# Two score products against one: the row maximum carried in spare rows of a matmul, with a full product ahead of it

## The chip, the cores and the metric

The kernel runs on one core of one Trainium2 chip. A core has a matrix engine (PE), a vector engine (DVE), a scalar engine that evaluates functions (ACT), a general engine (POOL, GpSimd), a queue that issues transfers (SP) and 16 DMA engines. Each has its own in-order instruction queue, and they meet through semaphores. The metric is device time in microseconds (us). All numbers are fp32.

## The reference, cut to what matters

A decoder of two layers works on 32 sequences of 128 tokens and width 128, each with its own context of 77 vectors. Each layer has a mixing step over the sequence, a cross-attention to the context and a mixture of experts, and a layer norm behind each. The change touches only the second layer's cross-attention, a differential attention with 16 heads, two queries and two keys of 4 dimensions per head, so 32 softmaxes per token:

```python
q = (query @ Wq.T).reshape(B, Nq, 2 * H, HD).transpose(0, 2, 1, 3)
k = (key_ @ Wk.T).reshape(B, Nk, 2 * H, HD).transpose(0, 2, 1, 3)
v = (value @ Wv.T).reshape(B, Nk, H, 2 * HD).transpose(0, 2, 1, 3)
a1 = softmax(q1 @ k1 * SCALE) @ v          # the first H of 2H heads
a2 = softmax(q2 @ k2 * SCALE) @ v          # the other H
attn = a1 - lam * a2                        # then normalised per head, scaled, @ Wp.T + bp
```

Each softmax takes the maximum of its 77 scores off before the exponential.

## The kernel before

The 32 sequences are handled in 8 groups of 4 (`G`). Everything is written with a tile framework: the Python code calls engines in an order of its own, generators are woven (`weave`, `beside`) so that parts of several stages alternate, and the framework then places each instruction in its engine's queue by priority and adds the semaphores. What stands first in a queue holds up what is behind it.

The second cross-attention is `cross1`, one generator over all 32 sequences (items). `beside(crossing, 6 * G, ...)` runs 24 steps of it per group and lets `before1(g + 1)` (gathering the experts' output in `combined`, the `memory` stage, then `prepare1`) and `after1(g - 1)` (`joined1`) take steps between. With group 2 done, the second half of the first layer's sorted experts is put in between (about 1010 to 1150 us).

`prepare1` makes, per group: the transposed queries (`dpq` in PSUM, copied by ACT to `dqT`, L753), the transposed keys (`dpk`, copied to `dkT`, L757), and per item the keys spread eight times with a mask (`km`, L763, on POOL): row group w (32 partitions) holds 8 of the 32 softmaxes, 4 rows each, and copy u of the keys is zero outside the 4 rows of softmax u. So copies 0 to 3 are zero in rows 16 to 31 of each row group, copies 4 to 7 in rows 0 to 15. The key dimension is padded from 77 to 78 by repeating the last one. `values` (L427, L435) makes the value operands `vb`.

An item passes through these steps, each for one half k (4 of the 8 softmaxes of each row group):

- `scores(n, k)`: four products (L784), one per row group, into four banks of PSUM; four DVE reductions (L786) write the maxima into `tops`, 8 used columns of 32 per row group.
- `by_query(n)`: PE transposes `tops` (`pt_mx`, L795), ACT copies it to `mT` (L797): now row 32w + u holds the maximum of softmax u for each query.
- `weights(n, k, mT)`: for each of three key thirds t and four row groups w, a product of keys and queries (L808, 32x104 stationary), and then, added onto the same place, a product (L819) of a constant selector `fold` (−1 where a key column belongs to softmax u) and `mT`. The sum is score minus maximum, keys on partitions. It lies in two PSUM tiles of two banks each (`dst`, pool `pair`, two buffers). ACT takes the exponential, one instruction per tile (L136 through `expln`, out `pT`).
- `reads(n, pTs, lhs, out)`: 12 products (L836) with `vb` or the mask `vmask` give numerators and denominators (`pav`), the item before being read while the present one is weighed.
- `difference`: reciprocal as exp(−ln) on ACT (`rd`), two DVE operations.

The PSUM pool `bank` has four buffers, shared by `dsc`, `pt_mx`, `dpq`, `dpk`, `pvc`, `pav` and others. The `prob` pool holds three `km` tiles of two items each.

Of the kernel before, what the change touches and what calls it, by code (L numbers as in the profile page):

```python
# [17 lines left out]
P = 128  # L18
# [33 lines left out]
def shape_constants():  # L52
    p = np.arange(P)
    cols = {}
    cols["ident"] = np.eye(P)
    cols["ones"] = np.ones((P, P))
    cols["before"] = (p[:, None] < p[None, :]) * 1.0
    cols["blk16"] = (p[:, None] // 16 == p[None, :] // 16) / 16.0
    cols["lag"] = np.maximum(p[None, :] - 1 - p[:, None], 0)
    cols["parity"] = np.broadcast_to(  # L60
        ((p[None, :] // 16) % 2 == np.arange(2)[:, None]).reshape(1, 2 * P), (P, 2 * P)
    )
    cols["qmask"] = (p[:, None] % 32) // 16 == np.arange(2)[None, :]
    cols["kmask0"] = ((p[:, None] % 32) // 8 == np.arange(4)[None, :]) / np.sqrt(8.0)
    cols["kmask1"] = ((p[:, None] % 32) // 4 == np.arange(8)[None, :]) * 0.5

    head, key = np.minimum(p // KT, 4), p % KT
    own = (head[:, None, None] == (np.arange(P) % 32 // 8)[None, None, :]) & ~(
        (np.arange(3) == 2)[None, :, None] & (key == KT - 1)[:, None, None]
    )  # L70
    cols["vmask"] = own.reshape(P, 3 * P)

    cols["fold"] = np.concatenate([p[:, None] % 32 == 4 * k + np.arange(4 * KT)[None, :] // KT for k in range(2)], axis=1) * -1.0
    cols["blk8"] = (p[:, None] // 8 == p[None, :] // 8) / 8.0
    cols["iota8"] = np.broadcast_to(np.arange(NE)[None, :], (P, NE))
    cols["iota32"] = np.broadcast_to(np.arange(32)[None, :], (P, 32))
    cols["before16"] = (p[:, None] // 16 == p[None, :] // 16) & (p[:, None] < p[None, :])
    cols["lower16"] = (p[:, None] // 16 < p[None, :] // 16) / 16.0
    cols["tile_no"] = np.broadcast_to(np.arange(NT)[None, :], (P, NT))
    cols["quad"] = p[:, None] // 32 == np.arange(4)[None, :]  # L80

    cols["token"] = p[:, None] + P * (2 * np.arange(16)[None, None, :] + np.arange(2)[None, :, None]).reshape(1, B)
    cols["eps"] = np.full((P, 1), EPS)
    at, parts, n = {}, [], 0
    for name, v in cols.items():
        v = np.asarray(v, np.float32)
        at[name] = (n, n + v.shape[1])
# [19 lines left out]
def kernel(ctx: ExitStack, tc: tile.TileContext, a: dict, at: dict):  # L107
# [57 lines left out]
    def c_(name):  # L165
        return cst[:, at[name][0] : at[name][1]]
# [6 lines left out]
        return vec[:, i : i + 1]  # L173

    ident, ones = c_("ident"), c_("ones")
    dmat = cp.tile([P, 8, P], F32, name="dmat")
    wv = cp.tile([P, 2, P], F32, name="wv")
    rows = cp.tile([P, 2, P], F32, name="rows")
# [568 lines left out]
    def prepare1(g, x4, c4):  # L747
        xT = transposed(x4, "c1")
        yield
        pq = bank("dpq")  # L750
        nc.tensor.matmul(pq, lhsT=w_("L1_xattn_Wq"), rhs=xT.rearrange("p b s -> p (b s)"), start=True, stop=True)
        qT = wk.tile([P, G, S], F32, tag="qT", name="dqT")
        nc.scalar.copy(qT, pq.rearrange("p (b s) -> p b s", b=G))  # L753
        pk = bank("dpk")[:, : G * S2]
        nc.tensor.matmul(pk, lhsT=w_("L1_xattn_Wk"), rhs=c4[:, :, 0, :], start=True, stop=True)
        kT = wk.tile([P, G, S2], F32, tag="ckT", name="dkT")
        nc.scalar.copy(kT, pk.rearrange("p (b k) -> p b k", b=G))  # L757
        yield
        km, vbs = [], []
        for b0 in range(0, G, 2):  # L760
            pair_km = wk.tile([P, 2, 8, S2], F32, tag="prob", bufs=3, name="km1")
            for i in range(2):
                nc.gpsimd.tensor_tensor(  # L763
                    pair_km[:, i],
                    kT[:, b0 + i, :].unsqueeze(1).broadcast_to([P, 8, S2]),
                    c_("kmask1").unsqueeze(2).broadcast_to([P, 8, S2]),
                    ALU.mult,
                )
                km.append(pair_km[:, i])
            for i in range(2):  # L770
                vbs.append(values(c4, b0 + i, 1))
            yield
        oT = wk.tile([P, G, S], F32, tag="oT", name="oT1")
        for b in range(G):
            operands[g * G + b] = qT[:, b, :], km[b], vbs[b], oT[:, b, :]
        held["oT", g] = oT

    def scores(n, k):

        qT, km, _, _ = operands[n]  # L780
        banks = [bank("dsc") for _ in range(4)]
        for w in range(4):
            rr = slice(32 * w, 32 * w + 32)
            nc.tensor.matmul(banks[w][:, : 4 * S2], lhsT=qT[rr], rhs=km[rr, 4 * k : 4 * k + 4, :], start=True, stop=True)  # L784
        for w in range(4):
            nc.vector.tensor_reduce(  # L786
                tops[n % 3][:, w, 4 * k : 4 * k + 4],
                banks[w][:, : 4 * S2].rearrange("p (h k) -> p h k", h=4),
                AX.X,
                ALU.max,  # L790
            )

    def by_query(n):
        pm = bank("pt_mx")[:, :P]
        nc.tensor.transpose(pm, tops[n % 3].rearrange("p w u -> p (w u)"), ident)  # L795
        mT = wk.tile([P, P], F32, tag="mT", name="mT")
        nc.scalar.copy(mT, pm)  # L797
        return mT

    def weights(n, k, mT):  # L800
        qT, km, _, _ = operands[n]
        pT = wk.tile([P, 2, 2, 3, S], F32, tag="pT", bufs=4, name="pT1")
        pts = [pair("dst") for _ in range(2)]
        fold = c_("fold")[:, k * 4 * KT : (k + 1) * 4 * KT]
        for t in range(3):
            for w in range(4):
                rr = slice(32 * w, 32 * w + 32)
                nc.tensor.matmul(  # L808
                    pts[w // 2][: 4 * KT, w % 2, t * S : (t + 1) * S],
                    lhsT=km[rr, 4 * k : 4 * k + 4, :].rearrange("p h k -> p (h k)")[:, t::3],  # L810
                    rhs=qT[rr],
                    start=(t == 0),
                    stop=False,
                    skip_group_check=True,
                )
        for t in range(3):
            for w in range(4):
                rr = slice(32 * w, 32 * w + 32)
                nc.tensor.matmul(  # L819
                    pts[w // 2][: 4 * KT, w % 2, t * S : (t + 1) * S],  # L820
                    lhsT=fold[rr],
                    rhs=mT[rr, :],
                    start=False,
                    stop=(t == 2),
                    skip_group_check=True,
                )
        for m in range(2):
            expln(pT[: 4 * KT, m].rearrange("p r t s -> p r (t s)"), pts[m][: 4 * KT, :, : 3 * S], AF.Exp)
        return pT
# [22 lines left out]
    def cross1():  # L852

        for n, k in ((0, 0), (0, 1), (1, 0)):
            scores(n, k)
            yield
        mT, past = by_query(0), None
        for n in range(B):
            pTs = [weights(n, 0, mT)]
            yield  # L860
            if past:
                acc = bank("pav1").rearrange("p (n m s) -> p n m s", n=2, m=2)
                reads(n - 1, past, operands[n - 1][2], acc[:, 0])
            yield
            if n + 1 < B:
                scores(n + 1, 1)
            yield
            pTs.append(weights(n, 1, mT))
            yield
            if past:  # L870
                reads(n - 1, past, vmask, acc[:, 1])
                difference(n - 1, acc)
            yield
            if n + 1 < B:
                mT = by_query(n + 1)
            if n + 2 < B:
                scores(n + 2, 0)
            yield
            past = pTs
        acc = bank("pav1").rearrange("p (n m s) -> p n m s", n=2, m=2)  # L880
        reads(B - 1, past, operands[B - 1][2], acc[:, 0])
        reads(B - 1, past, vmask, acc[:, 1])
        difference(B - 1, acc)
# [425 lines left out]
```

## Time and profile before

| what | value |
|---|---|
| three runs | 1725.04, 1725.79, 1734.47 us; median 1725.79 us |
| profiled execution | 1722.96 us, span 1721.2 us, mean granted PE clock 0.785 |
| PE busy (matmul) | 1309.1 us, 76% of the span |
| PE weight loads | 960.2 us, 56% |
| DVE / ACT / POOL busy | 767.3 (45%) / 461.1 (27%) / 544.0 (32%) us |
| instructions | 27680 |
| 882 to 985 us, PE busy, granted clock | 95.60 us, 0.96 |
| 1150 to 1470 us, PE busy, granted clock | 276.55 us, 0.88 |

How to read it: a line of the groups view has the code line, the engine, the operation, output<-inputs, shapes, the count, busy time and mean nanoseconds, and then the engine's idle time ahead of these instructions with what ended it. A timeline line has start, duration, engine, line and count, and in brackets the idle time before with its releaser. A window line has the stretch, its length, the busy time of PE, weight loads, DVE, ACT and POOL with counts, the granted PE clock as a share of full speed, the DMA share and GB/s. Each fp32 product of this kernel leaves two matmul records. Matmuls overlap, so that the sum of their durations is not the time PE is held; starts of neighbours tell that.

### The profile page before, as it was taken

The numbers are of one execution on the slowest core, as the hardware profiler recorded it, in microseconds if no ns is written. First come the engines' busy times: TensorE is split into PE (matmuls) and PEld (weight loads), VectorE is DVE, ScalarE is ACT, GpSimd is POOL, SyncE is SP. The second block draws the span as 40 slices with busy tenths as digits, with TensorE's granted clock in tenths as the row PEclk, the third lists the DMA queues.
The fourth block names the chain that finished last, engine by engine and source line by source line (L and its number), as shares of the span: only waits on it lengthen the run. The fifth ranks groups of instructions, "written<-read, shape, count | busy, mean of one in ns | idle before, by whom it ended". The sixth has DMA issues, their size and how long they took to land. (4 is left out here: it accounts for less than half of the span.)

```text
span 1721.2 us, 27680 instructions
## 1 busy us (share of the span) xinstructions
PE 1309.1 (76%) x11537; PEld 960.2 (56%) x11537; DVE 767.3 (45%) x2107; ACT 461.1 (27%) x928; POOL 544.0 (32%) x437
## 2 busy tenths in 40 slices
PE   5778877785677999678669999987889999425940
PEld 3555554554455888456336678865656666225520
DVE  3655556553555222676225532225355353472212
ACT  2222222221132333223023433323324333100213
POOL 0532424346643111652821101125121010004662
PEclk7966666666576999877679999998889998555885
DMA  8000000102200454110221026541110000001234
GB/s 244 20 22 19 20 18 21 26 11 70 80 19 7 144 186 151 50 34 25 82 70 35 14 71 195 172 137 44 28 40 14 16 14 14 16 0 27 54 30 109
DMA packets 122254, 100.98 MB, mean 59 GB/s; under 512 B 50064, under 2 KB 110224, under 8 KB 122128
## 3 DMA queue, kind: packets, MB, share of 16 engines
q1 hardware_dynamic: 105776, 50.30, 10.6%
q0 software_dynamic: 16352, 48.91, 9.9%
q8 instruction: 91, 1.49, 0.4%
q14 instruction: 35, 0.29, 0.1%
HBM read 72.29 MB, written 26.89 MB: 58 GB/s over the span
## 5 line engine op out<-in xcount | busy, mean ns | idle before, releaser
L669 PE MATMUL pgu<-tT,wt 128*128 128x256 f32 x736 | 172.0, 382 | 1.7 <-ACT tT L648 1.7
L786 DVE TENSOR_REDUCE top<-dsc 128x4 f32<-128x312 f32 x256 | 111.7, 475 | 122.8 <-PE dsc L784 115.5
L136 ACT ACTIVATE pT<-dst 104x768 f32<-104x768 f32 x128 | 96.7, 807 | 255.0 <-PE dst L819 205.0
L675 DVE TENSOR_TENSOR sg<-sg,pgu 128x512 f32<-128x512 f32 x92 | 63.3, 688 | 194.9 <-ACT sg L136 194.9
L669 PEld LDWEIGHTS pgu<-tT,wt 128*128 128x128 f32 x736 | 135.8, 192 | 18.2 <-ACT tT L648 2.2
L507 PE MATMUL ptp<-cst,prob 128*104 128x128 f32 x384 | 89.5, 410 | 73.3 <-POOL prob L497 60.6
L784 PE MATMUL dsc<-km,dqT 32*128 32x312 f32 x512 | 113.9, 503 | 29.6 <-DVE top L786 27.2
L494 POOL TENSOR_TENSOR prob<-prob,z 128x1248 f32<-128x1248 f32 x32 | 90.6, 2830 | 107.3 <-DVE z L493 103.1
L507 PEld LDWEIGHTS ptp<-cst,prob 128*104 128x104 f32 x384 | 70.8, 201 | 94.8 <-POOL prob L497 65.8
L808 PE MATMUL dst<-dqT,km 32*104 32x128 f32 x1536 | 117.4, 336 | 5.0 <-ACT pT L136 2.4
L654 POOL DMA_INDIRECT wt<-in_experts,which x46 | 43.9, 955 | 239.5 <-PE pd L679 226.9
L808 PEld LDWEIGHTS dst<-dqT,km 32*104 32x104 f32 x1536 | 97.6, 227 | 16.5 <-issue 7.4
L679 PE MATMUL pd<-wt,sg 128*128 128x128 f32 x736 | 99.6, 278 | 2.5 <-DVE sg L675 0.8
L679 PEld LDWEIGHTS pd<-wt,sg 128*128 128x128 f32 x736 | 93.1, 191 | 13.5 <-DVE sg L675 8.4
L784 PEld LDWEIGHTS dsc<-km,dqT 32*128 32x128 f32 x512 | 48.1, 195 | 79.0 <-DVE top L786 51.2
L819 PE MATMUL dst<-mT,cst 32*104 32x128 f32 x1536 | 87.0, 295 | 4.5 <-issue 4.4
L496 DVE TENSOR_REDUCE mx<-prob 128x16 f32<-128x1248 f32 x32 | 46.4, 1451 | 87.1 <-POOL prob L494 87.1
L497 POOL TENSOR_TENSOR prob<-prob,mx 128x1248 f32<-128x1248 f32 x32 | 72.9, 2279 | 38.4 <-DVE mx L496 36.6
L698 POOL DMA_INDIRECT two<-yslot,place x64 | 63.2, 988 | 67.7 <-DVE facc L705 29.7
L836 PE MATMUL pav<-pT,cst 104*32 104x256 f32 x768 | 65.6, 407 | 22.5 <-issue 21.7
L136 ACT ACTIVATE sg<-pgu 128x512 f32<-128x512 f32 x92 | 55.0, 597 | 95.5 <-PE pgu L669 95.5
L819 PEld LDWEIGHTS dst<-mT,cst 32*104 32x104 f32 x1536 | 77.0, 181 | 6.4 <-issue 6.4
(304 smaller groups left out, 2454.2 us busy)
## 6 DMA issues: line engine op xcount, KB each, us to landing
c<-in_ctxT SPq DMA_DIRECT2D x64, 156.0 KB
xslot<-zero SPq DMA_DIRECT2D x22, 256.0 KB
xs<-xslot SPq DMA_DIRECT2D x22, 256.0 KB
yslot<-y SPq DMA_DIRECT2D x22, 256.0 KB
wt<-in_experts SPq DMA_DIRECT2D x4, 768.0 KB
xg<-in_x SPq DMA_DIRECT2D x8, 256.0 KB
accrow<-fh SPq DMA_DIRECT2D x8, 256.0 KB
facc<-accrow SPq DMA_DIRECT2D x8, 256.0 KB
```

Of the source, the lines that this page charges most:

```text
L136: act = nc.scalar.activation(out, x, func, **kw)
L494: nc.gpsimd.tensor_tensor(ph, ph, z, ALU.add)
L497: nc.gpsimd.tensor_tensor(ph, ph, mx.unsqueeze(2).broadcast_to([P, 16, S2]), ALU.subtract)
L507: nc.tensor.transpose(pt[: 4 * KT, i, t * S : (t + 1) * S], ph[:, h0 : h0 + 4, :].rearrange("p h k -> p (h k)")[:, t::3], ident,)
L669: nc.tensor.matmul(pgu[:, i, c * TB * P : (c + 1) * TB * P], lhsT=w[:, at_w : at_w + P], rhs=x, start=True, stop=True)
L675: nc.vector.tensor_mul(flat, flat, pgu[:, 1, :])
L679: nc.tensor.matmul(pd[:, b, :], lhsT=sg[:, c, b, :], rhs=w[:, at_w : at_w + D], start=(c0 + c == 0 and b == 0), stop=(c0 + c == I0 // P - ...
L784: nc.tensor.matmul(banks[w][:, : 4 * S2], lhsT=qT[rr], rhs=km[rr, 4 * k : 4 * k + 4, :], start=True, stop=True)
L786: nc.vector.tensor_reduce(tops[n % 3][:, w, 4 * k : 4 * k + 4], banks[w][:, : 4 * S2].rearrange("p (h k) -> p h k", h=4), AX.X, ALU.max,)
L808: nc.tensor.matmul(pts[w // 2][: 4 * KT, w % 2, t * S : (t + 1) * S], lhsT=km[rr, 4 * k : 4 * k + 4, :].rearrange("p h k -> p (h k)")[:, t ...
L819: nc.tensor.matmul(pts[w // 2][: 4 * KT, w % 2, t * S : (t + 1) * S], lhsT=fold[rr], rhs=mT[rr, :], start=False, stop=(t == 2), skip_group ...
L836: nc.tensor.matmul(out[js], lhsT=lhs[: 4 * KT, t, js], rhs=pTs[j % 2][: 4 * KT, :, j // 2, t, :], start=(t == 0), stop=(t == 2), skip_grou ...
```

## The change

`weights` does one product in place of two. The masked keys `km` get −1 in one of the rows that were zero (a new constant `minus`), in row 16(1−k) + u mod 4; the queries are kept twice, each zeroed outside one half's 16 rows (`qz`, two ACT operations from PSUM), the maxima go to the matching columns of `tops`, and `by_query` adds the transposed maxima, masked to the other half's rows, to each half's queries (`qa`, two DVE operations straight from PSUM, in place of ACT's copy). So a row of −1 meets the row of the maximum within the same product. The key copies, with their scale and the −1 as bias, are made by ACT, 8 operations of 128x78 per item, in place of one POOL operation of 128x624. Ahead of each call's products, `busy` writes a product of the identity and 512 constant columns into the call's first bank; the real products overwrite what is read. The selector `fold` (208 columns) leaves the constants.

```diff
-    cols["fold"] = np.concatenate([p[:, None] % 32 == 4 * k + np.arange(4 * KT)[None, :] // KT for k in range(2)], axis=1) * -1.0
+    cols["minus"] = (p[:, None] % 32 == 16 * (1 - np.arange(8)[None, :] // 4) + np.arange(8)[None, :] % 4) * -1.0
...
+    def busy(banks):
+
+        for out in banks:
+            nc.tensor.matmul(out, lhsT=ident, rhs=cst[:, :512], start=True, stop=True)
...
-        qT = wk.tile([P, G, S], F32, tag="qT", name="dqT")
-        nc.scalar.copy(qT, pq.rearrange("p (b s) -> p b s", b=G))
+        qz = []
+        for k, tag in enumerate(("qT", "rq")):
+            qz.append(wk.tile([P, G, S], F32, tag=tag, name=f"dq{k}"))
+            nc.scalar.activation(
+                qz[k], pq.rearrange("p (b s) -> p b s", b=G), AF.Identity, bias=0.0, scale=c_("qmask")[:, k : k + 1]
+            )
...
-                nc.gpsimd.tensor_tensor(
-                    pair_km[:, i],
-                    kT[:, b0 + i, :].unsqueeze(1).broadcast_to([P, 8, S2]),
-                    c_("kmask1").unsqueeze(2).broadcast_to([P, 8, S2]),
-                    ALU.mult,
-                )
+                for u in range(8):
+                    nc.scalar.activation(
+                        pair_km[:, i, u, :], kT[:, b0 + i, :], AF.Identity,
+                        bias=c_("minus")[:, u : u + 1], scale=c_("kmask1")[:, u : u + 1],
+                    )
...
-            nc.tensor.matmul(banks[w][:, : 4 * S2], lhsT=qT[rr], rhs=km[rr, 4 * k : 4 * k + 4, :], start=True, stop=True)
+            nc.tensor.matmul(banks[w][:, : 4 * S2], lhsT=qz[k][rr], rhs=km[rr, 4 * k : 4 * k + 4, :], start=True, stop=True)
...
-                tops[n % 3][:, w, 4 * k : 4 * k + 4],
+                tops[n % 3][:, w, 16 * (1 - k) : 16 * (1 - k) + 4],
...
-        mT = wk.tile([P, P], F32, tag="mT", name="mT")
-        nc.scalar.copy(mT, pm)
-        return mT
+        qa = wk.tile([P, 2, P], F32, tag="mT", name="qa")
+        for k in range(2):
+            nc.vector.scalar_tensor_tensor(qa[:, k, :], pm, c_("qmask")[:, 1 - k : 2 - k], qz[k], ALU.mult, ALU.add)
+        return qa
...
         pts = [pair("dst") for _ in range(2)]
-        fold = c_("fold")[:, k * 4 * KT : (k + 1) * 4 * KT]
+        busy([pts[0][:, 0, :]])
         for t in range(3):
             for w in range(4):
                 rr = slice(32 * w, 32 * w + 32)
                 nc.tensor.matmul(
                     pts[w // 2][: 4 * KT, w % 2, t * S : (t + 1) * S],
                     lhsT=km[rr, 4 * k : 4 * k + 4, :].rearrange("p h k -> p (h k)")[:, t::3],
-                    rhs=qT[rr],
-                    start=(t == 0),
-                    stop=False,
-                    skip_group_check=True,
-                )
-        for t in range(3):
-            for w in range(4):
-                rr = slice(32 * w, 32 * w + 32)
-                nc.tensor.matmul(
-                    pts[w // 2][: 4 * KT, w % 2, t * S : (t + 1) * S],
-                    lhsT=fold[rr],
-                    rhs=mT[rr, :],
-                    start=False,
-                    stop=(t == 2),
-                    skip_group_check=True,
+                    rhs=qa[rr, k, :],
+                    start=True,
+                    stop=True,
                 )
```

More of the change, by code (lines that the diff above doesn't have):

```diff
@@ L774, in prepare1 @@
         for b in range(G):
-            operands[g * G + b] = qT[:, b, :], km[b], vbs[b], oT[:, b, :]
+            operands[g * G + b] = [q[:, b, :] for q in qz], km[b], vbs[b], oT[:, b, :]
         held["oT", g] = oT
     def scores(n, k):
-        qT, km, _, _ = operands[n]
+        qz, km, _, _ = operands[n]
         banks = [bank("dsc") for _ in range(4)]
@@ L793, in by_query, with weights @@
     def by_query(n):
+        qz, _, _, _ = operands[n]
         pm = bank("pt_mx")[:, :P]
         nc.tensor.transpose(pm, tops[n % 3].rearrange("p w u -> p (w u)"), ident)
-        mT = wk.tile([P, P], F32, tag="mT", name="mT")
-        nc.scalar.copy(mT, pm)
-        return mT
-    def weights(n, k, mT):
-        qT, km, _, _ = operands[n]
+        qa = wk.tile([P, 2, P], F32, tag="mT", name="qa")
+        for k in range(2):
+            nc.vector.scalar_tensor_tensor(qa[:, k, :], pm, c_("qmask")[:, 1 - k : 2 - k], qz[k], ALU.mult, ALU.add)
+        return qa
+    def weights(n, k, qa):
+        _, km, _, _ = operands[n]
         pT = wk.tile([P, 2, 2, 3, S], F32, tag="pT", bufs=4, name="pT1")
         pts = [pair("dst") for _ in range(2)]
-        fold = c_("fold")[:, k * 4 * KT : (k + 1) * 4 * KT]
+        busy([pts[0][:, 0, :]])
         for t in range(3):
@@ L856, in cross1 @@
             yield
-        mT, past = by_query(0), None
+        qa, past = by_query(0), None
         for n in range(B):
-            pTs = [weights(n, 0, mT)]
+            pTs = [weights(n, 0, qa)]
             yield
@@ L867, in cross1 @@
             yield
-            pTs.append(weights(n, 1, mT))
+            pTs.append(weights(n, 1, qa))
             yield
@@ L874, in cross1 @@
             if n + 1 < B:
-                mT = by_query(n + 1)
+                qa = by_query(n + 1)
             if n + 2 < B:
```

## The prediction

> **What bounds the kernel now.** I read the page's 40 slices first, to find the stage that the change touches. The tiles `dst`, `dsc` and `pT1` of the second cross-attention run from 770 to 1465 us, with the first layer's second half of sorted experts in the middle, and the rest of the kernel is untouched except for a constant. The costliest groups name what is removed:
>
> ```profile
> L808 PE MATMUL dst<-dqT,km 32*104 32x128 f32 x1536 | 117.4, 336 | 5.0 <-ACT pT L136 2.4
> L819 PE MATMUL dst<-mT,cst 32*104 32x128 f32 x1536 | 87.0, 295 | 4.5 <-issue 4.4
> L136 ACT ACTIVATE pT<-dst 104x768 f32<-104x768 f32 x128 | 96.7, 807 | 255.0 <-PE dst L819 205.0
> ```
>
> Each product leaves two records (64 calls of 12 products are 768, the rows say 1536). ScalarE's exponentials wait 205 us for PE and hardly the reverse: PE sets the pace. Its share from 1230 to 1465 us is 214.5 of 235 us, at a granted clock of 0.90. So I went to PE's timeline of one quiet half of an item (one `scores`, one `weights`, one `reads`):
>
> ```profile
> 1362.16 0.80 PE L784 MATMUL dsc<-km,dqT 32*128 32x312 f32 x6
> 1363.53 0.53 PE L784 MATMUL dsc<-km,dqT 32*128 32x312 f32 x1 [0.56 <-DVE top L786]
> 1363.53 0.56 PE L808 MATMUL dst<-dqT,km 32*104 32x128 f32 x6
> 1363.89 0.42 PE L784 MATMUL dsc<-km,dqT 32*128 32x312 f32 x1
> 1363.92 0.92 PE L808 MATMUL dst<-dqT,km 32*104 32x128 f32 x16
> ...
> 1365.72 1.50 PE L836 MATMUL pav<-pT,cst 104*32 104x256 f32 x24
> ```
>
> A half lasts about 5.1 us. See that the 4th score product and the first `dst` product start at the same 1363.53: they use different groups of 32 rows and run side by side. From there to the next stage, both products of `weights` take 2.19 us.
>
> **Part 1, the second product goes and a full one comes.** What 24 L819 records cost is best seen where `dst` follows a full product, and so is the price of `busy`:
>
> ```profile
> 1401.38 0.79 PE L784 MATMUL dsc<-km,dqT 32*128 32x312 f32 x2 [0.56 <-DVE top L786]
> 1402.10 1.97 PE L427 MATMUL pvc<-wv,c 128*104 128x128 f32 x12
> 1404.00 0.85 PE L808 MATMUL dst<-dqT,km 32*104 32x128 f32 x16
> 1404.68 0.83 PE L819 MATMUL dst<-mT,cst 32*104 32x128 f32 x24
> 1405.44 0.85 PE L836 MATMUL pav<-pT,cst 104*32 104x256 f32 x12
> ```
>
> ```profile
> 1246.10 1.02 PE L889 MATMUL prms<-sq,cst 128*128 128x512 f32 x2
> 1247.05 1.50 PE L836 MATMUL pav<-pT,vb 104*32 104x256 f32 x24
> ```
>
> L819 fills 1404.68 to 1405.44: 0.76 us. A full 128x512 product holds PE from 1246.10 to 1247.05: 0.95 us, 0.96 in another place. So the trade alone loses 0.20 us per call. In the quiet half it loses more, because the full product needs all rows: in the first fence here the next full product starts 1402.10 − 1401.38 = 0.72 us after the last score product, while `dst` starts after 0.00. The Trainium skill (TensorEngine Tiling, section Key Properties) says that a change of tiling mode drains the engine, which speaks against this change. By the naive sum a half would gain or lose only 0.96 − 0.76 = +0.20; with the drain it is 0.72 (drain) + 0.96 + 1.02 (24 L808 records from a fresh start: 16 in 0.68, 8 more at 0.043) = 2.70 against 2.19, +0.51 us. I take +0.51, bounds +0.20 and +0.80.
>
> The built order of the changed kernel says where the 64 full products stand: 31 directly behind four scores and ahead of `dst`, about 4 per group of 4 items. The other 4 are taken forward: behind the transposes `pt_mem` and behind `pr`, where before 8 L808 records (0.9 us) filled PE's wait for ScalarE, so that busy costs +0.06 there, 8 records return later (+0.35) and L819's 0.76 goes: −0.35 each; one behind `pt_mx` (+0.20); and one behind `pt_x`, counted in part 2. Per group: 4 × 0.51 − 2 × 0.35 = +1.3 us (the +0.20 behind `pt_mx` is covered by the wait of part 2).
>
> **Part 2, the key copies move from GpSimd to ScalarE.** GpSimd loses 32 L763 of 1251 ns, hidden. ScalarE gets 256 activations of 128x78 with two pointer operands. No such row exists; the nearest is L414/L286, 128x128 with both pointers, 481 ns; four of L286 in a row take 1.65 us, so (1.65 − 0.48)/3 = 0.39 us apart; less 50 elements at (807 − 597)/256 = 0.82 ns, 0.35 us apart. 32 make 11.2 us of ScalarE per group; bounds 0.30 and 0.40 each. ScalarE has the time (83 of 235 us busy), but its queue is in order. The built order is: scaled q twice, `dkT`, 13 copies, the two exponentials, 3 copies, the copy `xT_x`, 16 copies, a square-root pair, the next two exponentials. Before, it looked so:
>
> ```profile
> 1390.37 0.59 ACT L753 COPY dqT<-dpq 128x512 f32<-128x512 f32 x1
> ...
> 1390.96 0.41 ACT L757 COPY dkT<-dpk 128x312 f32<-128x312 f32 x1
> ...
> 1393.70 1.51 ACT L136 ACTIVATE pT<-dst 104x768 f32<-104x768 f32 x2 [2.17 <-PE dst L819]
> 1396.96 0.59 ACT L300 COPY xT_x<-pt_x 128x512 f32<-128x512 f32 x1 [1.75 <-PE pt_x L296]
> ```
>
> Now from 1390.4: two scaled copies of 0.69, 0.2 and 0.41 end at 1392.3; 13 × 0.35 end at 1396.9; the exponentials at 1398.4 (before 1395.2); 3 × 0.35 and `xT_x` at 1400.0 (before 1397.55); 16 × 0.35 at 1405.6, in time for the exponentials due at 1405.5. PE waits twice for this: `busy` for the bank of those exponentials, then the router's product L904 for `xT_x`, before at 1397.60, now 1400.0: +2.4 us, with all PE extras of that stretch inside. Behind it 22 `dst` records follow in place of 16 + 24 (1.0 against 1.44): −0.5. So +1.9 us per group; bounds 0 and +4.
>
> DVE gets two scalar_tensor_tensor per item (nearest L850, 343 ns): 0.7 us between the transpose and the first reduction, which today starts 1.08 us after the transpose does, so it fits in that gap; ScalarE loses the copy L797 (0.26). No queue is moved on SP; the constants shrink by 200 of 1986 columns (under 0.5 us at the start).
>
> Sum per group +1.3 + 1.9 = +3.2; seven groups prepared inside the crossing +22; group 0 has all 32 copies ahead of the first scores, where 4.8 us of GpSimd become 11.2 on ScalarE, of which items 0 and 1 are waited for: +3. Total about +25 us.
>
> **Credits.** (a) One L763 group sits inside GpSimd's chain of scatters, which holds PE back from 836 to 877 us:
>
> ```profile
> 824.44 0.97 POOL L624 DMA_INDIRECT xslot<-z,place  x1 [0.30 <-issue]
> 825.43 4.80 POOL L763 TENSOR_TENSOR km<-dkT,cst 128x624 f32<-128x624 f32 x4
> 830.40 1.00 POOL L624 DMA_INDIRECT xslot<-z,place  x1 [0.17 <-issue]
> ```
>
> −4.8, but two other operations (2.3) move in behind the first scatter; PE is fed slowly there (single records with "issue" gaps of 0.4 to 2.9) and has 48 L819 records less: −5 in all. (b) At 1202 and 1270 DVE stands before a DMA with PE's reductions behind it; in the built order those steps stand behind the next item's reductions: PE's waits of 2.98 + 3.22 become about 2.8, −3.4 each, −7. Net +25 − 12 = +13, on the profiled execution's 1722.96 us (span 1721.2): 1736; on the median of the runs, 1725.79, 2.8 us higher: 1739.
>
> **The clock.** What a full product could bring beside its cost is clock. The Trainium skill (TensorE: Matmul & The Clock Gate, Part 1) ties half rate to an idle window of about 3.4 us. By that rule it buys nothing in quiet halves, which run at 1.00, and nothing where PE is busy. But the windows show half rate with PE busy:
>
> ```profile
> 1338.00:1346.00 8.00, 7.44 (x76) 5.04 (x77) 2.86 (x6) 0.65 (x1) 0.00 (x0) 0.64 0.13 27
> 1346.00:1354.00 8.00, 7.33 (x121) 4.66 (x114) 3.49 (x9) 3.19 (x7) 0.00 (x0) 1.00 0.26 57
> ```
>
> PE is 7.44 of 8 us busy at 0.64. Summed over 8 us windows, 882 to 1466 us hold some 85 us at half rate; were they all full, 42 us would be gained. Most follow `pt_x`, where a full product now comes. By the rule 0, by the trace between 0 and −42. I take 0, since the +2.4 us wait falls in the same stretch.
>
> **The rivals.** (R1) *The full product holds the clock*: two thirds of those 85 us go, −28, and 13 − 28 = −15: 1711. For it: rows like 1338. Against: the stretch gets a longer wait. It ends on the other side; it decides once more than 45 us of half rate vanish (22 us of gain against +13 and the 0.5% bound). (R2) *ScalarE becomes the order that PE waits for*: copies at 0.40 us and exponentials behind 13 and 16 of them held at both places, +4 per group and +0.8 in the 32 quiet halves: +28 + 26 + 3 (group 0) − 5 (the filled waits) − 5 (credit a; b is lost) = +47: 1773. For it: in-order queue; against: 16.6 us of idle ScalarE in such a stretch at 1266. (R3) *The trade is level*: PE hides `busy` in the 0.56 us wait for `top`, copies fit: ±5, 1726. Against: `busy` stands behind the score that waits.
>
> **The numbers.** Mine 0.45, R1 0.20, R2 0.20, R3 0.15. Mine alone holds 1730 to 1752. A run-to-run difference of 0.5% (8.6 us) is about what a measurement can tell here. Faster: R1, 0.20. Same: R3 and the low edge of mine, 0.18. Slower 0.62. The range drops the outer half of R1 and of R2: 1708 to 1776.
>
> **What would show it.** `dst` of a quiet half 2.7 us after its last score; the full product 0.96 us; copies 0.35 us apart; `xT_x` about 2.4 us later relative to L904; PE's wait for ScalarE near 15 us more. Wrong if the granted clock from 1150 to 1470 rises well above 0.88, or if copies stretch past 0.40.

## The result, and the profile after

The changed kernel takes 1753.93 us, median of 4 runs (1751.38 to 1757.78), against 1725.41 in the runs beside it: a ratio of 1.0158, 95% interval 1.0123 to 1.0194. It is slower by about 28 us, where +13 was predicted. The profiled execution took 1755.67 us with a span of 1753.8, 32.6 more than before; all sums below are made against this span.

The groups of the page that answer to those of before (operation, shape and count, then busy time and mean of one, then the idle time before them):

```profile
L136 ACT ACTIVATE pT<-dst 104x768 f32<-104x768 f32 x128 | 96.9, 807 | 224.5 <-PE dst L819 183.3
L819 PE MATMUL dst<-qa,km 32*104 32x128 f32 x1536 | 94.3, 335 | 2.0 <-issue 1.9
L773 ACT ACTIVATE km<-dkT,cst 128x78 f32<-128x78 f32 x256 | 90.5, 456 | 0.4
L180 PE MATMUL dst<-cst 128*128 128x512 f32 x128 | 77.9, 693 | 6.4 <-ACT pT L136 6.4
```

L819 is now the only product of keys and queries into `dst` (it was L808 and L819, 117.4 and 87.0 us), L180 is the full product, L773 the key copies. ScalarE's exponentials still wait 183 us for TensorE, and the full product waits 6.4 us for ScalarE: TensorE sets the pace as before. Its timeline of one quiet half, one beside which nothing else is prepared (start, duration, then what was done):

```profile
1456.79 0.80 PE L792 MATMUL dsc<-km,dq 32*128 32x312 f32 x6
1458.15 0.79 PE L792 MATMUL dsc<-km,dq 32*128 32x312 f32 x2 [0.56 <-DVE top L794]
1458.87 1.12 PE L180 MATMUL dst<-cst 128*128 128x512 f32 x2
1459.93 1.14 PE L819 MATMUL dst<-qa,km 32*104 32x128 f32 x24
1460.99 1.50 PE L835 MATMUL pav<-pT,cst 104*32 104x256 f32 x24
...
```

From the last scores to the reads it takes 1460.99 − 1458.15 = 2.84 us (0.72 from the last score to the full product, then 1.06 and 1.06) where it took 2.19: +0.65 in each quiet half.

Where the 32.6 us lie is read from the 32 transposes `pt_mx`, one per item, whose start times divide the crossing in both traces (items are counted from 0):

| stretch | before | after | difference |
|---|---|---|---|
| start to item 0 | 775.1 | 777.5 | +2.4 |
| items 0 to 4 (with the scatters) | 116.6 | 116.7 | +0.1 |
| items 4 to 12 | 116.8 | 130.0 | +13.2 |
| items 12 to 13 (with the sorted experts) | 163.3 | 162.2 | −1.1 |
| items 13 to 31 | 285.8 | 303.5 | +17.7 |
| item 31 to the end | 263.5 | 263.9 | +0.4 |

A quiet item that waits for no gather goes from 10.24 to 11.53 us wherever it stands. The records of the granted clock say that half rate fills 20.5 us of items 4 to 12 after 3.4 before, and 63.1 after 60.5 in items 13 to 31. In items 4 to 12 that is already the sum: four quiet items make 5.2, and 17 us more at half rate cost up to 8.5, 13.7 against 13.2.

### The profile page after: what moved, and what is told of

It is laid out like the page before. It is cut to its first block, busy times and chain, and to the rows that moved or that the text cites. A ratio compares the mean times of both kernels' runs of the same rounds, so it can differ in the third digit from the quotient of the medians.

```text
span 1753.8 us, 25103 instructions
## 1 busy us (share of the span) xinstructions
PE 1347.8 (77%) x10129; PEld 934.5 (53%) x10129; DVE 773.5 (44%) x2171; ACT 550.7 (31%) x1160; POOL 503.8 (29%) x405
## 3 DMA queue, kind: packets, MB, share of 16 engines
q8 instruction: 80, 1.31, 0.3%
## 5 line engine op out<-in xcount | busy, mean ns | idle before, releaser
L792 PE MATMUL dsc<-km,dq 32*128 32x312 f32 x512 | 131.3, 523 | 46.7 <-DVE top L794 33.5
L680 DVE TENSOR_TENSOR sg<-sg,pgu 128x512 f32<-128x512 f32 x92 | 63.3, 688 | 194.8 <-ACT sg L136 194.8
L792 PEld LDWEIGHTS dsc<-km,dq 32*128 32x128 f32 x512 | 53.2, 200 | 107.4 <-DVE top L794 54.0
L819 PEld LDWEIGHTS dst<-qa,km 32*104 32x104 f32 x1536 | 78.3, 231 | 41.5 <-issue 39.9
L819 PE MATMUL dst<-qa,km 32*104 32x128 f32 x1536 | 94.3, 335 | 2.0 <-issue 1.9
L773 ACT ACTIVATE km<-dkT,cst 128x78 f32<-128x78 f32 x256 | 90.5, 456 | 0.4
L180 PE MATMUL dst<-cst 128*128 128x512 f32 x128 | 77.9, 693 | 6.4 <-ACT pT L136 6.4
L136 ACT ACTIVATE pT<-ptp 104x768 f32<-104x768 f32 x64 | 51.8, 811 | 92.8 <-PE ptp L512 89.1
```

Source lines behind the costliest of these rows:

```text
L136: act = nc.scalar.activation(out, x, func, **kw)
L180: nc.tensor.matmul(out, lhsT=ident, rhs=cst[:, :512], start=True, stop=True)
L680: nc.vector.tensor_mul(flat, flat, pgu[:, 1, :])
L773: nc.scalar.activation(pair_km[:, i, u, :], kT[:, b0 + i, :], AF.Identity, bias=c_("minus")[:, u : u + 1], scale=c_("kmask1")[:, u : u + 1],)
L792: nc.tensor.matmul(banks[w][:, : 4 * S2], lhsT=qz[k][rr], rhs=km[rr, 4 * k : 4 * k + 4, :], start=True, stop=True)
L819: nc.tensor.matmul(pts[w // 2][: 4 * KT, w % 2, t * S : (t + 1) * S], lhsT=km[rr, 4 * k : 4 * k + 4, :].rearrange("p h k -> p (h k)")[:, t ...
```

## The experiments

All are compared with the kernel before in the same runs. They come from two chips: in the first four experiments the kernel before takes 1724.82 us, in the later ones 1714.16 and 1713.17. The changed kernel's first trace and its later one differ by 13 us in items 0 to 4 and by less than 1 us in items 4 to 12 and 13 to 31, so times are compared by ratio, and traces in these two stretches. "Half rate" is the time at half clock within items 4 to 12 plus 13 to 31 (63.9 us before, 83.6 in the changed kernel). The expectations name larger sums for it (102, 180, 99, 78), because the records of the clock had been laid some 20 us too late on the trace; their order is the same.

### The two parts taken apart: four kernels

**The full product left out.**

```diff
         pts = [pair("dst") for _ in range(2)]
-        busy([pts[0][:, 0, :]])
         for t in range(3):
```

> The changed kernel without the full product; the single product and the key copies on ScalarE stay. Cost theory (the full product costs its 1.06 us and a drain of 0.72 us in each of some 31 quiet halves, and holds no clock): a half gets 1.2 to 1.7 us shorter, 31 x 1.45 = 45, so about 1709 us, between 1700 and 1718. Clock theory (R1, the full product holds the clock): what is won in the halves is lost in half rate, 1735 or more, and the half-rate time from 900 us on grows well beyond the 102 us of the changed kernel. ScalarE theory (R2, the copies set the pace): 1745 or more.

Measured: 1727.58 us, ratio 1.0024 (0.9994 to 1.0054). The quiet half, TensorE's timeline:

```profile
1443.39 0.53 PE L792 MATMUL dsc<-km,dq 32*128 32x312 f32 x1 [0.56 <-DVE top L794]
1443.39 0.56 PE L818 MATMUL dst<-qa,km 32*104 32x128 f32 x6
1443.75 0.42 PE L792 MATMUL dsc<-km,dq 32*128 32x312 f32 x1
1443.78 1.21 PE L818 MATMUL dst<-qa,km 32*104 32x128 f32 x18
1444.92 1.50 PE L834 MATMUL pav<-pT,cst 104*32 104x256 f32 x24
```

The last score and the first `dst` product start together again, and the reads come after 1.53 us: the full product costs 1.31 us in a quiet half. Yet only 26 us came back where the cost theory asked for 45, because half rate grew from 83.6 to 158.3 us. Both theories are half right: the full product costs what its place on TensorE says, and it does hold the clock, which pays some 15 us of the price back (an estimate: 31 × 1.31 = 41, less 26).

**The full product added to the kernel before.**

```diff
         pts = [pair("dst") for _ in range(2)]
+        busy([pts[0][:, 0, :]])
         for t in range(3):
```

> The kernel before, with only the full product added ahead of the first product into dst; the second product and the copies on GpSimd stay. Cost theory: the quiet half goes from 2.19 to 0.72 + 1.06 + 1.04 + 0.76 = 3.58 us between last score and reads, 32 x 1.4 = +44, about 1770. Clock theory: the gain in clock pays it back, 1745 or less.

Measured: 1762.60 us, ratio 1.0224 (1.0179 to 1.0268), +38. Quiet items last 12.84 us, 2.60 more than before, again 1.30 per half. Half rate falls from 63.9 to 44.3 us, worth up to 10 us. From the four kernels the terms of a quiet half can be read alone: the full product +1.30 (11.53 − 8.93 = 2.60 and 12.84 − 10.24 = 2.60 per item), the second product −0.65 (10.24 − 8.93 = 1.31 per item).

**The key copies back on GpSimd**, as the product of before and one addition of the spare rows.

```diff
-                for u in range(8):
-                    nc.scalar.activation(
-                        pair_km[:, i, u, :], kT[:, b0 + i, :], AF.Identity,
-                        bias=c_("minus")[:, u : u + 1], scale=c_("kmask1")[:, u : u + 1],
-                    )
+                nc.gpsimd.tensor_tensor(
+                    pair_km[:, i],
+                    kT[:, b0 + i, :].unsqueeze(1).broadcast_to([P, 8, S2]),
+                    c_("kmask1").unsqueeze(2).broadcast_to([P, 8, S2]),
+                    ALU.mult,
+                )
+                nc.gpsimd.tensor_tensor(
+                    pair_km[:, i], pair_km[:, i],
+                    c_("minus").unsqueeze(2).broadcast_to([P, 8, S2]),
+                    ALU.add,
+                )
```

> The changed kernel with the key copies back on GpSimd: one product with the mask as before and one addition of the spare rows, 128x624 each, in place of 8 activations per item; the full product stays. My part 2 (1.9 us per group and 3 for the first) gives -16, 1738. If only what the trace of the changed kernel shows as waits for ScalarE in the crossing (6.4 + 3.6 us) goes: -5 to -10, 1744 to 1749. R2 (ScalarE is the order that TensorE waits for): 1725 or less.

Measured: 1729.57 us, ratio 1.0020 (1.0003 to 1.0036): the copies on ScalarE cost 24 us by the medians (18.8 by the two traces, since this run's profiled execution is 7.5 us above its median), more than part 2 had (16) and far more than TensorE's visible waits for ScalarE (10 us). Half rate is 59.2 us, 24 less.

**Both edits.**

> Both edits: no full product, key copies on GpSimd (product and addition). If the two costs stand side by side: the sum of the two single differences, about 1754 - 45 - 8 = 1701. If without the full product the copies on ScalarE become the pace, this is better than the sum: 1690. If GpSimd's two operations of 1.25 us each per item come too late: above the kernel without the full product alone.

Measured: 1703.85 us, ratio 0.9894 (0.9860 to 0.9927), faster than the kernel before. The two prices add up: 1.0024 + 1.0020 − 1.0158 = 0.9886. What is left, the single product with its spare rows, is the change's gain, about 18 us; the full product takes 1.3% of the time back and the copies on ScalarE 1.4%. The gain is what is left after a loss of clock: half rate is 117.3 us here, 63.9 in the kernel before.

### What the full product costs: stream or drain

**Four products of 32 rows in place of one of 128.**

```diff
-        busy([pts[0][:, 0, :]])
+        for w in range(4):
+            rr = slice(32 * w, 32 * w + 32)
+            nc.tensor.matmul(pts[w // 2][:, w % 2, :], lhsT=ident[rr], rhs=cst[rr, :512], start=True, stop=True)
```

> The changed kernel with the full product cut into four products of 32 rows and 512 columns, one per group of 32 rows into the bank that the group's products use, so that nothing changes its tiling between scores and dst. The same number of columns streams, and the rows stay as busy. Without the full product a quiet half takes 1.30 us less (8.93 against 11.53 us per item in the two traces), while the stream is 1.06. If the drain costs the remaining 0.24 us: quiet item 11.05, and 30 of these halves give -7 to -10, 1745. If the stream is all: quiet item 11.5 and 1754. If the four products can't run side by side: a quiet item of 14 us or more and 1790.

Measured: 1791.30 us, ratio 1.0452 (1.0401 to 1.0502), a miss for the whole and an answer for the part. A quiet item takes 10.65 us, (10.65 − 8.93) / 2 = 0.86 per half for the stream alone, so 1.30 − 0.86 = 0.44 us of the full product's price is that it can't run beside the 32-row products around it. The whole got slower for another reason: with more products to place, the built order put 20 key copies (13 in the changed kernel) ahead of the exponentials of a preparation, TensorE waited for ScalarE 13.6 + 5.5 us, and half rate rose to 143 us; the two items beside a preparation took 22 and 25 us, 3.5 and 5 more.

**Half its width.**

```diff
-        busy([pts[0][:, 0, :]])
+        nc.tensor.matmul(pts[0][:, 0, :256], lhsT=ident, rhs=cst[:, :256], start=True, stop=True)
```

> The changed kernel with the full product at 256 in place of 512 columns. If the stream sets its price: 0.50 us less per half, quiet item 10.5 us, and over the 30 halves where it is not hidden -15, less a few us of clock given back: 1740 to 1746. If its price is a fixed one of standing there: quiet item 11.5, 1754. If only the rate of work that it brings holds the clock: half-rate time in the crossing grows from 102 towards 180 us.

Measured: 1716.09 us, ratio 1.0016 (1.0000 to 1.0031), 24 us better than the full width by the ratios. Quiet items take 10.68 us, −0.43 per half, so 512 columns stream in 0.86 us and 0.44 us are fixed, the same split as above. Half rate is 85.7 us, no more than with the full width. Of the 24 us, the sixteen quiet items explain 14; of the rest 6 lie in items 0 to 4, among the scatters (97.8 us against 103.7 in the changed kernel's second trace below), and aren't explained.

### The copies on ScalarE, and the clock behind a wait

**The copies alone, in the kernel before.**

```diff
-                nc.gpsimd.tensor_tensor(
-                    pair_km[:, i],
-                    kT[:, b0 + i, :].unsqueeze(1).broadcast_to([P, 8, S2]),
-                    c_("kmask1").unsqueeze(2).broadcast_to([P, 8, S2]),
-                    ALU.mult,
-                )
+                for u in range(8):
+                    nc.scalar.activation(
+                        pair_km[:, i, u, :], kT[:, b0 + i, :], AF.Identity,
+                        bias=0.0, scale=c_("kmask1")[:, u : u + 1],
+                    )
```

> The kernel before with one edit: the masked keys are written by 8 activations on ScalarE per item (scale only, no spare rows) in place of one product on GpSimd; both products into dst stay, and no full product comes. My part 2: 7 x 1.9 + 3 = +16, 1741. As the changed kernel has it against the run with its copies on GpSimd (2.2 us of waits and 2.1 us of half rate behind them, per group): +21 to +30, 1746 to 1755. R2 (ScalarE is the order that TensorE waits for in quiet halves too): 1770 or more. Quiet items must stay at 10.24 us if the price lies in the preparations alone.

Measured: 1755.71 us, ratio 1.0240 (1.0190 to 1.0289), +41. Quiet items that wait for no gather stay at 10.24 us: none of it lies there. ScalarE's timeline and, below it, TensorE's:

```profile
1428.95 6.87 ACT L764 ACTIVATE km<-dkT,cst 128x78 f32<-128x78 f32 x27
1435.72 1.49 ACT L136 ACTIVATE pT<-dst 104x768 f32<-104x768 f32 x2
1437.10 1.11 ACT L764 ACTIVATE km<-dkT,cst 128x78 f32<-128x78 f32 x4
1438.10 0.58 ACT L300 COPY xT_x<-pt_x 128x512 f32<-128x512 f32 x1
```

```profile
1436.57 1.45 PE L807 MATMUL dst<-dqT,km 32*104 32x128 f32 x10 [2.83 <-ACT pT L136]
1438.73 1.88 PE L903 MATMUL pl<-router,xT_x 128*128 128x8 f32 x8 [0.71 <-ACT xT_x L300]
...
1446.57 2.89 PE L427 MATMUL pvc<-wv,c 128*104 128x128 f32 x12
```

Here 27 copies stand ahead of the exponentials, and TensorE waits 2.83 + 0.71 us. But pvc takes 2.89 us, where it takes 1.97 at full rate. The records of the clock show why: all stretches of half rate begin on a fixed grid of 3.41 us and last a multiple of it. The same stretch of the trace cut on that grid (length, then busy time and instructions of TensorE, its weight loads, VectorE, ScalarE, GpSimd; then the clock, the DMA share and the rate):

```profile
1428.80:1432.20 3.40, 3.40 (x62) 3.14 (x60) 2.51 (x8) 3.40 (x15) 1.27 (x1) 1.00 0.43 127
1432.20:1435.60 3.40, 1.54 (x12) 1.30 (x11) 1.11 (x2) 3.40 (x15) 0.00 (x0) 1.00 0.13 34
1435.60:1439.00 3.40, 1.72 (x12) 1.13 (x12) 0.00 (x0) 3.34 (x9) 0.00 (x0) 0.51 0.00 0
1439.00:1442.40 3.40, 3.40 (x28) 2.46 (x32) 0.21 (x1) 0.00 (x0) 0.00 (x0) 0.50 0.00 0
1442.40:1445.80 3.40, 2.84 (x19) 1.06 (x12) 1.10 (x3) 0.00 (x0) 0.00 (x0) 0.50 0.00 0
1445.80:1449.20 3.40, 3.40 (x14) 2.56 (x12) 1.21 (x3) 0.00 (x0) 0.00 (x0) 0.50 0.00 0
```

In the second window TensorE is busy 1.54 of 3.40 us, still at full rate; then come four windows at half, two of them wholly busy. Counted over the fourteen profiles of this case, 890 to 1490 us: after a window at full rate in which TensorE was busy less than 50%, the next was at half in 61 of 61; at 50 to 70% in 81 of 108; at 70 to 85% in 33 of 283; above 85% in 11 of 1513. So a wait of some 1.5 us inside one window is mostly paid twice: once as the wait, and then as half rate.

Busy time only stands in for something else: the work done in the window. Take each product record as the columns that it streams times the share of the 128x128 array that its tile covers (0.20 for 32x104), and split a record that crosses an edge in proportion to its time. The two records of a full 128x512 product are 1024 such columns, the 24 records of the removed second product 624. After one of the same windows at full rate with less than 1300 columns of work, the next was at half in 142 of 142; with 1300 to 1400 in 35 of 36; with 1400 to 1600 in 9 of 62; with more in 0 of 1725. This sorts what busy time does not: eight windows that TensorE filled to 96% or more still lost the clock, with 1302 to 1424 columns, and the 27 of the 50 to 70% band that kept it had 1452 or more. It also says when full rate returns: a window at half with less than 1300 columns was followed by another at half in 267 of 269, one with 1300 to 1600 in 35 of 147, one with more in 0 of 65. The second window above has 1197. This is a count over kernels built for other questions; no run was made to vary the work alone.

**Half of the copies on GpSimd** (of each pair the second item; the first keeps its 8 activations).

```diff
             for i in range(2):
-                for u in range(8):
-                    nc.scalar.activation(...)
+                if i == 0:
+                    for u in range(8):
+                        nc.scalar.activation(...)
+                else:
+                    nc.gpsimd.tensor_tensor(pair_km[:, i], ..., ALU.mult)
+                    nc.gpsimd.tensor_tensor(pair_km[:, i], pair_km[:, i], ..., ALU.add)
```

> The changed kernel with half of the key copies (one of the two items of each pair) moved to GpSimd as product and addition. In the built order 13 activations still stand ahead of the two exponentials of each preparation, as in the changed kernel, but only 3 behind in place of 19. If the place in ScalarE's queue is what costs (13 x 0.35 = 4.6 us of copies ahead of exponentials that have 2.3 us of room): no gain beside the changed kernel on the same chip, within 5 us. If the amount of copies counts: half of the gain of the run with all copies on GpSimd, -12.

Measured: 1720.62 us, ratio 1.0051 (1.0032 to 1.0069), 16 us less than the changed kernel beside it (1737.06). The theory of the place in the queue falls. The waits for ScalarE did stay (6.3 + 5.0 us), yet most of the gain came, and it came as clock: half rate 37.5 us against 86.2. The same place of a preparation in the changed kernel and, below it, in this one, cut on their grids:

```profile
1423.60:1427.00 3.40, 2.65 (x15) 1.66 (x13) 1.11 (x2) 3.40 (x9) 0.00 (x0) 1.00 0.05 12
1427.00:1430.40 3.40, 2.81 (x35) 2.00 (x34) 0.21 (x1) 3.40 (x11) 0.00 (x0) 1.00 0.00 0
1430.40:1433.90 3.50, 2.93 (x16) 1.03 (x9) 1.26 (x3) 3.21 (x10) 0.00 (x0) 0.52 0.00 0
1433.90:1437.30 3.40, 3.40 (x25) 3.14 (x28) 1.53 (x3) 0.00 (x0) 0.00 (x0) 0.50 0.00 0
```

```profile
1393.00:1396.40 3.40, 2.60 (x17) 2.32 (x18) 1.49 (x3) 3.40 (x9) 3.40 (x4) 1.00 0.24 72
1396.40:1399.80 3.40, 2.68 (x28) 1.52 (x30) 0.21 (x1) 1.82 (x5) 0.48 (x1) 1.00 0.00 0
1399.80:1403.20 3.40, 2.84 (x25) 1.50 (x18) 1.74 (x4) 0.00 (x0) 0.00 (x0) 1.00 0.00 0
```

TensorE's busy times are alike (2.65 and 2.81 against 2.60 and 2.68), both in the band where 33 of 283 windows lose the clock; the changed kernel has 14 stretches of half rate in items 4 to 12 and 13 to 31, this one 5. By work they differ: the changed kernel's first two windows have 2244 and 1311 columns, this kernel's three 2099, 1607 and 1497. In the whole band the 33 windows that lost the clock had at most 1436 columns, and the 250 that kept it at least 1463.

**A quarter of the copies on ScalarE** (the first item of the group alone, by `if b0 + i == 0:` in the same place).

> The changed kernel with a quarter of the key copies (8 activations, one item of the group) on ScalarE and the other items' on GpSimd. 8 copies stand ahead of the two exponentials, 2.8 us against 2.3 us of room. If the place in the queue costs by what exceeds the room: the whole gain of the run with all copies on GpSimd, -21 to -25 beside the changed kernel on the same chip, half rate from the 13th item on near 61 us. If the amount counts: three quarters, -18, which this can't tell apart, but the waits for ScalarE would then be a quarter of 10 us and not zero.

Measured: 1716.03 us, ratio 1.0021 (1.0009 to 1.0033), 21 us less than the changed kernel beside it, the whole gain of moving all copies. The waits for ScalarE are 2.2 + 0.7 us, half rate 55.4.

**The changed kernel again**, beside these two and the one below.

> The changed kernel as it is, on the chip of the three runs beside it, as their reference: 1.4% to 1.8% slower than the kernel before on the same chip.

Measured: 1737.06 us, ratio 1.0151 (1.0124 to 1.0177); half rate 86.2 us. From item 4 on its stretches repeat the first trace (129.8, 159.7 and 302.6 us); items 0 to 4 take 103.7 us in place of 116.7.

### Where the full product pays

**Only beside the preparations**, with the copies on GpSimd.

```diff
-        busy([pts[0][:, 0, :]])
+        if n % G in (1, 2):
+            busy([pts[0][:, 0, :]])
```

> Key copies on GpSimd (product and addition, as in the run before), and the full product only in two of four items, those beside which the next group is prepared; the two quiet items of each group have none. If the full product is hidden in the preparations and holds the clock there: quiet items at 8.93 us, half rate in the crossing near the 78 us of the run with all full products, and 1685 to 1695, better than 1704 without any. If the clock depends on the whole stretch, quiet items too: half rate near 127 us and 1704 or more. If the full product costs its 1.3 us in the preparations as well: about 1715.

Measured: 1685.88 us, ratio 0.9842 (0.9794 to 0.9889): 1.6% faster than the kernel before, the lowest ratio of all. Its interval overlaps that of the kernel without any full product (0.9860 to 0.9927), so the times alone don't show a gain over that one; the two traces point to one. Quiet items are at 8.9 us, and half rate in items 13 to 31 is 43.0 us against 85.7 without any full product; this stretch takes 266.4 us against 276.3 without and 291.4 with all of them.

**Only in the quiet items** (`n % G in (0, 3)`).

> The opposite placement to the run with the full product in the preparations alone: key copies on GpSimd, full product only in the two quiet items of each group. If the full product costs 1.3 us per quiet half and holds the clock only where TensorE waits: quiet items at 11.5 us, half rate from the 13th item on near the 99 us of the run without any (54.6 with it in the preparations), and about +35 us beside that placement, 0.6% to 1.2% slower than the kernel before. If the clock goes by the work over a longer stretch: half rate near 60 us, and +10 to +20 beside it.

Measured: 1703.26 us, ratio 0.9946 (0.9929 to 0.9963), 1.0% behind the other placement. Quiet items are at 11.5 us, as expected, but half rate in items 13 to 31 is 35.4 us, lower still: the clock is held from here too, so "only where TensorE waits" was wrong. With full products in both places and the copies on GpSimd it was about 49 us. So either place alone holds the clock at least as well as both, and the second one pays its price without winning more of it: if the two effects added, both together would be at 0.9842 + 0.9946 − 0.9894 = 0.9894, and they measured 1.0020. The longest stretch of half rate in these items is 10.2 us with either placement and 30.7 us without any full product. It fits the counts of work: a window at half that takes in a full product comes sooner to the columns that end it. That is argued; no run isolates it.

## Why the prediction was wrong

The direction and the range held; the size did not, +13 against 28 (32.6 in the profiled span). That 1754 us lies in the range speaks for its width, drawn to take in R1 and R2, and not for the steps: a loss of clock that it put at nothing, and credits that never came. By its own steps:

**Part 1, +0.51 per quiet half: right in kind, too small.** The drain was 0.72 and a fresh `dst` 1.06 (1.02 predicted), but the full product holds TensorE for 1.06 us between these products and not 0.96. +0.65 instead, inside the bounds; over 31 halves 4 us more. The −0.35 for each product taken forward behind `pt_mem` and `pr` can't be seen: the items beside a preparation without other disturbance (5, 9, 17, 21) changed by −0.2, +1.2, −0.3 and +1.1.

**Part 2, the waits: right, and smaller.** Copies are 0.35 us apart, as estimated, and 13, 2, 3, 1 and 16 follow each other as in the built order. ScalarE's timeline of one preparation in the changed kernel, and TensorE's below it:

```profile
1420.62 4.59 ACT L773 ACTIVATE km<-dkT,cst 128x78 f32<-128x78 f32 x13
1425.10 1.49 ACT L136 ACTIVATE pT<-dst 104x768 f32<-104x768 f32 x2
1426.48 1.14 ACT L773 ACTIVATE km<-dkT,cst 128x78 f32<-128x78 f32 x3
1427.51 0.58 ACT L305 COPY xT_x<-pt_x 128x512 f32<-128x512 f32 x1
1427.98 5.63 ACT L773 ACTIVATE km<-dkT,cst 128x78 f32<-128x78 f32 x16
```

```profile
1425.95 1.13 PE L180 MATMUL dst<-cst 128*128 128x512 f32 x2 [0.75 <-ACT pT L136]
...
1428.14 1.06 PE L903 MATMUL pl<-router,xT_x 128*128 128x8 f32 x8 [0.59 <-ACT xT_x L305]
...
1433.88 2.89 PE L432 MATMUL pvc<-wv,c 128*104 128x128 f32 x12
```

TensorE waits 0.75 + 0.59 = 1.34 us here, where +2.4 − 0.5 was predicted; all its waits for `pT` and `xT_x` in the crossing are 10.0 us after 3.4, so 6.6 more, where 15 more had been named. But the pvc at the end, 2.89 us in place of 1.97, shows the price that the step left out: half rate. With it the copies cost 24 us.

**The clock, taken as 0: the first step that failed.** The prediction weighed a row at half rate with TensorE 93% busy against a rule of the Trainium skill (TensorE: Matmul & The Clock Gate, Part 1) of an idle window of about 3.4 us, and took 0 because the longer wait falls in the same stretch; its bounds (0 to −42) reached to the side of a gain alone. The runs show the window's length, 3.41 us, but not that it must be idle. The row that was shown is the tail of a stretch at half rate, and the window ahead of that stretch, in the kernel before, was this:

```profile
1333.50:1336.90 3.40, 3.02 (x36) 2.35 (x40) 1.77 (x6) 1.35 (x3) 2.27 (x2) 1.00 0.00 0
```

TensorE is busy for 89% of it, and yet the next two windows are at half: by work it has 1124 columns, under the 1300 below which every counted window lost the clock. In the changed kernel the copies' waits take work out of such windows, and the term became a loss: 24 us more half rate from item 0 to 31 (177.5 against 153.5), up to 12 us. The sign that was named, the granted clock from 1150 to 1470 us, stayed at 0.88 and could not show it: most of the growth (17 us) lies in items 4 to 12.

**The credits, −12: the second step that failed; none came.** (a) L763 did leave the chain of scatters on GpSimd, and two other operations came in, as said. But the chain also began later, because its first index came later from VectorE. GpSimd's timeline:

```profile
821.71 1.09 POOL L659 DMA_INDIRECT wt<-in_experts,which  x1 [16.35 <-DVE place L618]
823.11 1.00 POOL L629 DMA_INDIRECT xslot<-z,place  x1 [0.30 <-issue]
...
838.17 1.05 POOL L740 TENSOR_TENSOR my<-x 128x512 f32<-128x512 f32 x1
...
844.22 1.28 POOL L895 TENSOR_TENSOR c1xb<-x,rows 128x512 f32<-128x512 f32 x1
```

In the kernel before, the first scatter was this:

```profile
820.57 1.00 POOL L624 DMA_INDIRECT xslot<-z,place  x1 [0.30 <-issue]
```

So the chain begins 2.5 us later: −4.8 + 2.3 + 2.5 = 0, and the last scatter starts at 864.8 in both traces. (b) The two waits of TensorE that were to shrink stood so in the kernel before:

```profile
1201.86 2.79 PE L836 MATMUL pav<-pT,vb 104*32 104x256 f32 x24 [2.98 <-DVE vb L435]
...
1209.21 1.40 PE L784 MATMUL dsc<-km,dqT 32*128 32x312 f32 x2 [3.22 <-DVE top L786]
```

The first was for the value operands `vb` and not for a reduction, as the prediction had it. VectorE's waits for gathers didn't go; they moved into the next quiet item. VectorE's timeline in the changed kernel, and TensorE's score behind it:

```profile
1310.54 0.35 DVE L710 SCALAR_TENSOR_TENSOR facc<-two,share,facc 128x128 f32<-128x128 f32 x1 [2.51 <-DMA two<-yslot,place]
1311.92 0.35 DVE L710 SCALAR_TENSOR_TENSOR facc<-two,share,facc 128x128 f32<-128x128 f32 x1 [1.03 <-DMA two<-yslot,place]
1313.11 0.35 DVE L710 SCALAR_TENSOR_TENSOR facc<-two,share,facc 128x128 f32<-128x128 f32 x1 [0.84 <-DMA two<-yslot,place]
1313.38 0.48 DVE L794 TENSOR_REDUCE top<-dsc 128x4 f32<-128x312 f32 x1
```

```profile
1313.91 0.87 PE L792 MATMUL dsc<-km,dq 32*128 32x312 f32 x2 [4.18 <-DVE top L794]
```

From item 13 to item 16 it takes 63.3 us after 54.8, and from 17 to 20 55.0 after 54.6, where 3.4 less had been forecast for each.

**The sum** is then 13 + 12 (credits) + up to 12 (clock) + 4 and 5 (part 1: the larger half, and seven times the two gains of 0.35 that don't show) − 7 (waits of part 2, 6.6 us for seven times 1.9): up to 39 against 32.6. The 3 us for group 0 fit the +2.4 ahead of item 0. The clock's share is an upper end, since half rate costs nothing where TensorE waits anyway; how much less it was can't be read from these traces, and so the sum is closed no better than this.

**The rivals.** R1's mechanism exists (half rate 158.3 against 83.6 us without and with the full product, 117.3 against 59.2 with the copies on GpSimd), but its price of 1.30 us per quiet half is higher than what it wins. R2 is right that the copies are a main cost (24 us), and wrong in its place: TensorE waits for them in no quiet half. R3 is out.

## What to carry to other kernels

Cost a wait on TensorE twice: once as itself, and once as the clock that it may take. To see whether it takes it, add up the work in the window around it (columns times the share of the array), not the busy time. Work that only keeps the clock pays its price in every place and wins clock once: here the same product lost 1.3% over all items, lost 0.5% in the quiet ones and, by the medians, won 0.5% (0.9842 against 0.9894, with intervals that overlap) beside the preparations. A credit for work that leaves an in-order chain counts only once the chain's start and its next input have been followed too.

## What the runs showed of the hardware

Half rate comes in steps of 3.41 us on a fixed grid. It follows a window with too little work on TensorE, where a small tile counts by its share of the array: under 1300 columns in all of 142 cases, over 1600 in none of 1725. It ends by the same count (the next window was at half again in 267 of 269 and in 0 of 65). A full 128x512 product between 32-row products costs 1.30 us: 0.86 of stream and 0.44 of standing alone (from the quiet items of the kernels with four products and with half the width, which agree). Key copies of 128x78 on ScalarE go out every 0.35 us with a pointer for both scale and bias, and every 0.25 us with a scale alone (27 in 6.87 us), so the second pointer costs 0.10 us on each.
